# One stacked float32r product for the first feed-forward layer, finer steps beside the attention rounds, and a gather that turns two images' choices at once

## The chip, the cores and the metric

The kernel runs on one core of a Trainium2 chip. The core has a matrix engine (PE, with its weight loads PEld), a vector engine (DVE), a scalar engine for activation functions (ACT), a general engine (POOL) and SyncE (SP), which here only issues DMAs. Each engine works off its own list of instructions in order; they meet at semaphores. PE writes into PSUM[...]; the other engines read it from there. The metric is the device time of one execution in microseconds. The kernel before was timed three times: 11410.22, 11418.36 and 11421.47 us, median 11418.36.

## The reference

Four images of 64 x 64 tokens with 128 channels go through a layer of three state-space scans (forward, backward, and across slices) and then through a transformer block with a mixture of experts. What the change touches is in the second part. With 16 heads of size 8 and 4096 tokens per image:

```python
qkv = _qz_ring(heads + rx_theta)                     # q = k = v, products of cosines
scores = einsum('bhsd,bhtd->bhst', q, q) / sqrt(8)
ctx = einsum('bhst,bhtd->bhsd', softmax(scores), q)
x1 = _ln(x + ctx @ w_comb.T + b_comb, g1, beta1)
zf = cos(x1[..., :8]) * cos(ry_theta)                # 8 values a token
h = relu(zf @ w1.T + b1)                             # 8 -> 512
x2 = _ln(x1 + h @ w2.T + b2, g2, beta2)              # 512 -> 128
```

and then, on the layer norm of the sum, the experts:

```python
probs = softmax(x @ gate_w.T + gate_b, axis=tokens)  # 64 experts, each over an image's tokens
topv, topi = top_k(probs, 8)                         # 8 tokens for each expert
pooled = sum_k topv * x[topi]                        # one vector per expert and image
out = weight2(gelu(weight1(pooled)))                 # each expert's two layers
outputs[topi] += topv * out
```

## The kernel before, in words

`tile_kernel` (from L1522 on) runs in stages: the scan of image 0 beside the inputs of all images; the opening of image 0's attention; four attention loops, one per image; and a closing.

**A loop.** `loop` works through 1024 rounds (4 groups of heads x 8 query blocks x 32 key chunks). Round i issues, in this order: the four score products of round i+1 (L998, float32r, 32 rows each) with two exps of 128 x 1024 on ACT (L1003); then `beside(i)`, the place for other work; then the four value products of round i (L1012, 32 columns each, float32). PE takes them in that order, so a product that is put in by `beside` stands between the scores of the next round and the values of this one. For the first three images the scan of the next image and its opening run there, and `after` of the image before. For the last image, `by_block` is set: the rounds run query block by query block, and `self.whole[b]` counts the blocks whose context is stored.

**What runs beside the last loop**, chained in one `Pace`: `after(2)` (all eight blocks of image 2), the expert biases, search, choice and gather of images (0, 1), the same of image 2, then `after(3)` for blocks 0-3, 4-5 and 6 of image 3, each of which waits for `whole`, and the search over those seven blocks. What is left when the rounds are over is issued by `last.rest()`; then block 7 is closed (`closing`, on 7 PSUM banks), followed by choice and gather of image 3 and the experts' answers. During the loops there is a single PSUM bank for all work beside (`Bank`, size 1).

**The pace.** The parts are generators. A `yield` ends a step; `yield PE` says that the next step has PE work. In the last loop `turn(1.5, free)` allows 1.5 steps a round on average (three saved up at most), of which one PE step if `free` is true; that is `i % 3 > 0 or i > 830`. `bank.take` yields PE once. `pause()` yields PE only where `self.cut` is set, which is in the last loop.

**A block of 512 tokens.** `first(g)`: context times its share, two halves of two products with `w_comb` (`co`, L1115), norm, the first 8 channels copied to `z`. `cosines()`: range reduction on DVE and the sine on ACT, for all blocks of the call. `second(g)`: four transposes of `z` (`zt`, L1138), scaling by `cos_ry` into `zT` (8 x 512), eight products with `w1` (`h`, L1156), relu on DVE (on ACT in the closing), sixteen products with `w2` (`fo`, L1169), two norms (L878 to L884), four transposes (`xT`, L1193), two gate products (`lg`, L1207). `flow` interleaves two blocks.

**The gather.** `pool(b, g)` handles one image and four chunks of tokens: four products that turn the chosen weights (`wt`, L1342, 64 rows by 64 columns), a copy, four products with the tokens (`pool`, L1353), an addition into `pooled`.

Of the kernel before, what the change touches and what calls it, by code (L numbers as in the profile page):

```python
# [713 lines left out]
class Attention:  # L714
# [3 lines left out]
    def __init__(self, tc, ctx, w, gate, cols, ident, bank, dram, t1, w_out, scans, sz, x):  # L718
# [16 lines left out]
        self.cos_ry = const.tile([D, 3], F32, name="cos_ry")  # L735
        nc.scalar.dma_start(out=self.cos_ry[:, 0:1], in_=w["ry_theta"].unsqueeze(1))
        cosine(nc, self.cos_ry[:, 2:3], self.cos_ry[:, 0:1], self.cos_ry[:, 1:2], self.half_pi)
        self.w_comb = const.tile([P, C], F32, name="w_comb")
        self.w1 = const.tile([D, FFN], F32, name="w1")
# [6 lines left out]
        with tc.tile_pool(name="a_load", bufs=1) as load, tc.tile_pool(  # L746
# [8 lines left out]
            nc.sync.dma_start(out=raw, in_=w["w1"].rearrange("(f p) d -> p f d", p=P))  # L755
            ps = load_ps.tile([P, 512], F32, tag="ps", name="ps_w1")
            for f in range(4):
                nc.tensor.transpose(ps[:D, f * P : (f + 1) * P], raw[:, f, :], ident)
            nc.vector.tensor_copy(self.w1, ps[:D])
# [299 lines left out]
    def after(self, b, gs=range(L // QB), to=None):  # L1059
# [13 lines left out]
        z = self.small.tile([P, NT, D], F32, tag="z", bufs=1, name=f"z_{b}_{gs[0]}")  # L1073

# [20 lines left out]
        def first(g):  # L1095
# [32 lines left out]
        def second(g):  # L1128
# [12 lines left out]
            nc.vector.tensor_scalar_mul(zT, ps[:D], self.cos_ry[:, 2:3])  # L1141
# [8 lines left out]
            for f in range(4):  # L1150
                ps = yield from self.bank.take(f"h_{b}_{g}_{f}")
                for part in range(2):
                    cols = slice(part * QB // 2, (part + 1) * QB // 2)
                    if part:
                        yield from self.pause()
                    nc.tensor.matmul(ps[:, cols], self.w1[:, f * P : (f + 1) * P], zT[:, cols], start=True, stop=True)  # L1156
# [63 lines left out]
        def cosines():  # L1220
            turns = self.small.tile([P, NT, D], F32, tag="zturns", bufs=1, name=f"zturn_{b}_{gs[0]}")
            zs, turns = (t[:, 4 * gs[0] : 4 * blocks.stop, :] for t in (z, turns))
# [4 lines left out]
            yield  # L1227
            yield
# [10 lines left out]
class Experts:  # L1239
# [4 lines left out]
    def __init__(self, tc, ctx, ident, weight1, weight2, block, nb):  # L1244
# [14 lines left out]
        self.diagonal = const.tile([P, nb // 2, E], F32, name="diagonal")  # L1259
# [40 lines left out]
    def choice(self, images, blocks):  # L1300
# [24 lines left out]
        for b in images:  # L1325
            own = slice(b % 2 * E, b % 2 * E + E)
            nc.vector.tensor_scalar_mul(
                self.diagonal[own, b // 2, :], self.ident[own, own], self.share[own, b // 2 : b // 2 + 1]
# [4 lines left out]
    def pool(self, b, g):  # L1333

        nc, bank, rows = self.nc, self.block.bank, slice(b % 2 * E, b % 2 * E + E)
        x = self.some.tile([P, 4, C], F32, tag="x", bufs=4, name=f"x_{b}_{g}")
        nc.sync.dma_start(out=x, in_=self.block.xn[b][:, g * 4 : g * 4 + 4, :])
        yield
        ps = yield from bank.take(f"wt_{b}_{g}")
# [7 lines left out]
        wT = self.some.tile([P, 4, E], F32, tag="wT", name=f"wT_{b}_{g}")  # L1347
        nc.vector.tensor_copy(wT.rearrange("p i e -> p (i e)"), ps[:, : 4 * E])
        bank.leave()
        yield  # L1350
        ps = yield from bank.take(f"pool_{b}_{g}")
        for i in range(4):
            nc.tensor.matmul(ps[:, :E], x[:, i, :], wT[:, i, :], start=(i == 0), stop=(i == 3))  # L1353
        yield
        into = self.pooled[:, :, b]
        if g == 0:
            nc.vector.tensor_copy(into, ps[:, :E])
        else:
            nc.vector.tensor_add(into, into, ps[:, :E])
        bank.leave()  # L1360
        yield
# [310 lines left out]
```

## Time and profile before

The profiled execution took 11412.32 us, of which its instructions span 11410.5.

| stretch, us from the start | what | ACT busy | PE busy | PE clock |
|---|---|---|---|---|
| 0 to 2047 | scan of image 0, inputs, opening of image 0 | | | |
| 2047 to 4426 | loop of image 0 | 2321.2 of 2379 | 2128.9 | 0.98 |
| 4428 to 6794 | loop of image 1 | 2304.5 of 2366 | 2138.9 | 0.98 |
| 6799 to 9124 | loop of image 2 | 2266.7 of 2325 | 2117.2 | 0.98 |
| 9126 to 11162 | loop of image 3 | 1925.4 of 2036 | 1964.3 | 0.98 |
| 11162 to 11228 | closing of block 7 | 4.4 of 66 | 19.0 | 0.59 |
| 11228 to 11282 | choice and gather of image 3 | 6.1 of 54 | 31.1 | 0.50 |
| 11282 to 11411 | experts and output | 20.2 of 129 | 72.9 | 0.91, then 0.67 |

The busy time of PE counts pipelined products, so a high share does not say that PE is at its peak. ACT's busy time in the loops is nearly all exps: 2048 of them in 1904.7 us in the last loop. The first three loops carry the exps of a scan on ACT as well. The products of the last loop's other work, by PE's groups between 9126 and 11162: `fo` 85.4 us (240 products), `h` 72.2 (120), `wt` 28.2, `pool` 26.5, `co` 22.5, `lg` 19.4, `xT` 14.4, `zt` 12.1. A float32 product has two records in the trace, so its count there is twice the number of products.

### The profile page before, as it was taken

What the parts mean: (1) busy time and instruction counts of PE and PEld (TensorE: products, weight loads), DVE (VectorE), ACT (ScalarE), POOL (GpSimd) and SP (SyncE); (2) the same over time, 40 slices, a digit from 0 to 9 for tenths busy, and PEclk for the clock granted to TensorE, in tenths of its full rate; (3) what the DMA queues carried; (4) which work ended last, traced back from release to release, by engine and by line L of the source; (5) the groups of instructions that cost most, each with busy time, mean ns of one, the idle gap of its engine ahead of it and who ended that gap; (6) DMA issues with size and microseconds to landing.
All of it is one profiled execution on the core that took longest, in us unless ns stands there. A gap on an engine that the chain in (4) does not pass through costs nothing.

```text
span 11410.5 us, 183033 instructions
## 1 busy us (share of the span) xinstructions
PE 9874.3 (87%) x68358; PEld 3273.6 (29%) x68358; DVE 8258.3 (72%) x8405; ACT 9993.7 (88%) x10828; POOL 3790.3 (33%) x3891
## 2 busy tenths in 40 slices
PE   6687792788998889899998899999998999999995
PEld 2233331222222222222222222222222223333323
DVE  6889997888888987999988979988998321111212
ACT  4566672899999999999999999999999999989992
POOL 4777784332323223424333124243331110000000
PEclk8798895899999999999999999999999999999997
DMA  6778897656565665665656755656556332222225
GB/s 188 226 231 230 226 249 198 161 145 156 142 155 155 178 174 146 158 154 142 151 147 160 194 157 156 156 141 151 146 147 162 116 100 72 76 71 84 75 65 186
DMA packets 900980, 1747.52 MB, mean 153 GB/s; under 512 B 203150, under 2 KB 443846, under 8 KB 899830
## 3 DMA queue, kind: packets, MB, share of 16 engines
q1 hardware_dynamic: 764734, 1469.68, 47.9%
q0 software_dynamic: 93856, 156.41, 4.8%
q10 hardware_dynamic: 41496, 109.71, 3.6%
q8 instruction: 537, 8.80, 0.3%
q14 instruction: 357, 2.92, 0.1%
HBM read 1379.76 MB, written 355.47 MB: 152 GB/s over the span
## 4 chain that ended last, share of the span: by engine, by line
PE 38%; ACT 24%; issue 14%; DVE 11%; DMA 10%; POOL 1%; SPq 1%; ACTq 0%; DVEq 0%; POOLq 0%
PE acc L1012 21%; ACT e L1003 20%; PE s L998 10%; DVE h L561 5%; DMA delta<-d_delta 4%; PE cv L412 2%; DMA du<-d_du 2%; DVE dB L551 1%; ACT dA L542 1%; PE y L599 1%; ACT delta L542 1%; PE fo L1169 1%; PE xd L426 1%; PE h L1156 1%; DMA w<-in_L_ffn_weight_dram 1%
## 5 line engine op out<-in xcount | busy, mean ns | idle before, releaser
L1003 ACT ACTIVATE e<-s 128x1024 f32<-128x1024 f32 x8192 | 7778.1, 1105 | 234.2 <-PE s L998 222.2
L1012 PE MATMUL acc<-e,val 128*32 128x512 f32 x32768 | 5250.2, 615 | 106.5 <-ACT av L1021 93.7
L998 PE MATMUL s<-qm,key 32*128 32x512 f32 x16384 | 2650.8, 501 | 588.8 <-ACT e L1003 558.9
L998 PEld LDWEIGHTS s<-qm,key 32*128 32x128 f32 x16384 | 1013.4, 184 | 4444.4 <-issue 2483.9
L563 POOL COPY ends<-h 128x1 f32<-128x1 f32 x1152 | 1333.8, 1159 | 2362.4 <-DVE h L561 2353.2
L551 DVE TENSOR_TENSOR dB<-du,B 128x1024 f32<-128x1024 f32 x960 | 1213.6, 1264 | 441.2 <-PE y L599 217.2
L1012 PEld LDWEIGHTS acc<-e,val 128*32 128x32 f32 x32768 | 973.5, 109 | 1608.4 <-issue 789.0
L561 DVE TENSOR_TENSOR_SCAN h<-dA,ends,dB 128x1024 f32<-128x1024 f32 x576 | 1351.2, 2346 | 110.3 <-ACT dA L542 66.2
L542 ACT ACTIVATE dA<-delta,A 128x1024 f32<-128x1024 f32 x768 | 935.7, 1218 | 500.5 <-DMA delta<-d_delta 460.8
L561 DVE TENSOR_TENSOR_SCAN h<-delta,ends,du 128x1024 f32<-128x1024 f32 x432 | 1013.2, 2345 | 127.2 <-ACT delta L542 64.3
L568 POOL TENSOR_TENSOR hC<-h,C 128x1024 f32<-128x1024 f32 x384 | 993.5, 2588 | 153.3 <-PE y L599 83.7
L542 ACT ACTIVATE delta<-delta,A 128x1024 f32<-128x1024 f32 x768 | 937.4, 1221 | 7.3 <-DVE dB L551 2.2
L572 DVE TENSOR_TENSOR du<-h,C 128x1024 f32<-128x1024 f32 x576 | 702.2, 1219 | 0.1
L572 DVE TENSOR_TENSOR dB<-h,C 128x1024 f32<-128x1024 f32 x576 | 702.2, 1219 | 0.0
L551 DVE TENSOR_TENSOR du<-du,B 128x1024 f32<-128x1024 f32 x576 | 691.6, 1201 | 5.8 <-DMA B<-d_bc 5.8
L1027 POOL DMA_DIRECT2D d_ctx<-av x512 | 260.3, 518 | 1026.1 <-DVE av L1021 647.6
L412 PE MATMUL cv<-xn,conv 128*128 128x512 f32 x1024 | 469.7, 612 | 26.8 <-DVE xn L346 17.2
L593 POOL DMA_DIRECT2D d_du<-x_delta x272 | 157.2, 578 | 1003.0 <-DVE x_delta L592 945.1
L561 DVE TENSOR_TENSOR_SCAN h<-dA,dB 128x1024 f32<-128x1024 f32 x192 | 438.9, 2286 | 50.3 <-ACT dA L542 40.9
L599 PE MATMUL y<-hC,sel 128*32 128x256 f32 x3072 | 247.8, 456 | 171.7 <-DVE o L615 160.0
L599 PE MATMUL y<-dB,sel 128*32 128x256 f32 x4608 | 378.8, 401 | 9.9 <-DVE xT L1196 4.8
L561 DVE TENSOR_TENSOR_SCAN h<-delta,du 128x1024 f32<-128x1024 f32 x144 | 329.1, 2285 | 68.3 <-issue 35.0
(246 smaller groups left out, 7200.5 us busy)
## 6 DMA issues: line engine op xcount, KB each, us to landing
delta<-d_delta SPq DMA_DIRECT2D x768, 512.0 KB
du<-d_du SPq DMA_DIRECT2D x576, 512.0 KB
du<-d_du ACTq DMA_DIRECT2D x192, 512.0 KB
key<-d_q SPq DMA_DIRECT2D x352, 256.0 KB
d_u<-u SPq DMA_DIRECT2D x48, 1024.0 KB
d_delta<-r SPq DMA_DIRECT2D x48, 1024.0 KB
B<-d_bc SPq DMA_DIRECT2D x96, 512.0 KB
C<-d_bc SPq DMA_DIRECT2D x96, 512.0 KB
```

The source lines that it names most:

```text
L412: nc.tensor.matmul(banks[2 * m + g], w["conv"][:, k, m * P : (m + 1) * P], reads(k, g), start=(k == 0), stop=(k == 3))
L542: nc.scalar.activation(tiles["delta", s], t, AF.Exp, scale=A)
L551: nc.vector.tensor_mul(tiles["du", s], du, spread[order, c, "B", j % 2])
L561: nc.vector.tensor_tensor_scan(h, dA, dB, first, ALU.mult, ALU.add)
L563: nc.gpsimd.tensor_copy(ends[order, c][:, at : at + 1], h[:, T - 1 :])
L568: nc.gpsimd.tensor_mul(tiles["du", s], h, spread[order, c, "C", j % 2])
L572: nc.vector.tensor_mul(dB, h, spread[order, c, "C", j % 2])
L599: nc.tensor.matmul(y[32 * g : 32 * g + 32, : T // 4], self.sel[:, j // 2, :], hC[:, 256 * g : 256 * g + 256], start=(j == 0), stop=(j == 3),)
L998: nc.tensor.matmul(s_ps[:, k, :], keys[f"{i // 4}"][rows, cut].bitcast(F32R), queries[j, qb][rows, :].bitcast(F32R), start=True, stop=True,)
L1003: nc.scalar.activation(e, s_ps, AF.Exp, scale=1.0 / math.sqrt(D))
L1012: nc.tensor.matmul(accs[j, qb][32 * k : 32 * k + 32, :], v[:, k * VW : k * VW + 32], es[i][k // 2][:, k % 2, :], start=(kc == 0), stop=(kc ...
L1027: nc.gpsimd.dma_start(out=self.context[b][h * D : h * D + D, cut], in_=av[32 * k : 32 * k + D, :])
```

## The change

It has three parts.

1. The first feed-forward product. Each of `zf` and `w1` is split into a high part (the upper bits, by a mask) and a low part (the rest)[...]. They are stacked to 32 rows, `z` as high, low, high, low and `w1` as high, high, low, low. One float32r product of 32 rows and 512 columns then gives what two float32 products of 256 columns gave. `cos_ry` is multiplied into `z` before the split, by DVE in `cosines()`, rather than by the copy out of PSUM; the transposes `zt` now bring 32 rows.
2. Pauses. Inside the last loop `co` is put in one product at a time rather than two, `fo` one rather than two, and `wt` and `pool` two rather than four. The `h` product needs no pause any more.
3. The gather takes the pair of images (0, 1) in one call: `wt` uses 128 rows and 128 columns (a diagonal of 128) and makes the turned weights of both, and `pool` then follows for each image.

```diff
+def split(nc, to, src):
+    bits = mybir.dt.uint32
+    nc.vector.tensor_single_scalar(to[0].bitcast(bits), src.bitcast(bits), HIGH, ALU.bitwise_and)
+    nc.vector.tensor_sub(to[1], src, to[0])
...
-        self.w1 = const.tile([D, FFN], F32, name="w1")
+        self.w1 = const.tile([4 * D, FFN], F32, name="w1")
...
+        parts = self.one.tile([P, NT, 4, D], F32, tag="zparts", bufs=1, name=f"zparts_{b}_{gs[0]}")
...
                 for k in range(2):
+                    if k:
+                        yield from self.pause()
                     at = slice((2 * half + k) * P, (2 * half + k + 1) * P)
                     nc.tensor.matmul(ps[:, k * C : (k + 1) * C], cT[:, at], self.w_comb, start=True, stop=True)
...
-                nc.tensor.transpose(ps[:D, k * P : (k + 1) * P], z[:, g * 4 + k, :], self.ident)
+                nc.tensor.transpose(
+                    ps[: 4 * D, k * P : (k + 1) * P], parts[:, g * 4 + k, :, :].rearrange("p x d -> p (x d)"), self.ident
+                )
             yield
-            zT = self.piece([D, 512], "p0", name=f"zT_{b}_{g}")
-            nc.vector.tensor_scalar_mul(zT, ps[:D], self.cos_ry[:, 2:3])
+            zT = self.piece([4 * D, 512], "p0", name=f"zT_{b}_{g}")
+            nc.vector.tensor_copy(zT.bitcast(F32R), ps[: 4 * D])
...
-                for part in range(2):
-                    cols = slice(part * QB // 2, (part + 1) * QB // 2)
-                    if part:
-                        yield from self.pause()
-                    nc.tensor.matmul(ps[:, cols], self.w1[:, f * P : (f + 1) * P], zT[:, cols], start=True, stop=True)
+                nc.tensor.matmul(
+                    ps, self.w1[:, f * P : (f + 1) * P].bitcast(F32R), zT.bitcast(F32R), start=True, stop=True
+                )
...
                 for f in range(4):
-                    if f == 2:
+                    if f:
                         yield from self.pause()
                     nc.tensor.matmul(
                         ps[:, :C], h[:, f, k * P : (k + 1) * P], self.w2[:, f, :], start=(f == 0), stop=(f == 3)
...
             nc.scalar.activation(zs, zs, AF.Sin, bias=self.half_pi, scale=-1.0)
             yield
+            yield
+            n = zs.shape[1]
+            four = parts[:, 4 * gs[0] : 4 * blocks.stop, :, :]
+            nc.vector.tensor_mul(zs, zs, self.cos_ry[:, 2, :].unsqueeze(1).to_broadcast([P, n, D]))
+            split(nc, (four[:, :, 0, :], four[:, :, 1, :]), zs)
+            nc.vector.tensor_copy(four[:, :, 2:, :], four[:, :, :2, :])
             yield
...
-    def pool(self, b, g):
+    def pool(self, images, g):
...
         for i in range(4):
             at = (g * 4 + i) * P
+            if i == 2:
+                yield from pause()
             nc.tensor.matmul(
-                ps[:, i * E : (i + 1) * E], self.chosen[b // 2][rows, at : at + P], self.diagonal[rows, b // 2, :],
+                ps[:, i * n : (i + 1) * n], self.chosen[j][rows, at : at + P], self.diagonal[rows, j, rows],
                 start=True, stop=True,
             )
...
+        for k, (b, x) in enumerate(zip(images, xs)):
+            ps = yield from bank.take(f"pool_{b}_{g}")
+            for i in range(4):
+                if i == 2:
+                    yield from pause()
+                nc.tensor.matmul(ps[:, :E], x[:, i, :], wT[:, i, k * E : (k + 1) * E], start=(i == 0), stop=(i == 3))
...
     def gather(self, images):
-        yield from flow((self.pool(b, g) for b in images for g in range(NT // 4)), 2, 3)
+        yield from flow((self.pool(images, g) for g in range(NT // 4)), 2, 3)
```

More of the change, by code (lines that the diff above doesn't have):

```diff
@@ L734, in __init__ @@
         nc.scalar.dma_start(out=self.b1, in_=w["b1"].rearrange("(f p) -> p f", p=P))
-        self.cos_ry = const.tile([D, 3], F32, name="cos_ry")
-        nc.scalar.dma_start(out=self.cos_ry[:, 0:1], in_=w["ry_theta"].unsqueeze(1))
-        cosine(nc, self.cos_ry[:, 2:3], self.cos_ry[:, 0:1], self.cos_ry[:, 1:2], self.half_pi)
+        self.cos_ry = const.tile([P, 3, D], F32, name="cos_ry")
+        nc.scalar.dma_start(out=self.cos_ry[:, 0, :], in_=w["ry_theta"].partition_broadcast(P))
+        cosine(nc, self.cos_ry[:, 2, :], self.cos_ry[:, 0, :], self.cos_ry[:, 1, :], self.half_pi)
         self.w_comb = const.tile([P, C], F32, name="w_comb")
-        self.w1 = const.tile([D, FFN], F32, name="w1")
+        self.w1 = const.tile([4 * D, FFN], F32, name="w1")
         self.w2 = const.tile([P, 4, C], F32, name="w2")
@@ L755, in __init__ @@
             nc.sync.dma_start(out=raw, in_=w["w1"].rearrange("(f p) d -> p f d", p=P))
+            parts = load.tile([P, 4, 4, D], F32, name="parts_w1")
+            split(nc, (parts[:, :, 0, :], parts[:, :, 2, :]), raw)
+            nc.vector.tensor_copy(parts[:, :, 1, :], parts[:, :, 0, :])
+            nc.vector.tensor_copy(parts[:, :, 3, :], parts[:, :, 2, :])
             ps = load_ps.tile([P, 512], F32, tag="ps", name="ps_w1")
             for f in range(4):
-                nc.tensor.transpose(ps[:D, f * P : (f + 1) * P], raw[:, f, :], ident)
-            nc.vector.tensor_copy(self.w1, ps[:D])
+                nc.tensor.transpose(
+                    ps[: 4 * D, f * P : (f + 1) * P], parts[:, f, :, :].rearrange("p x d -> p (x d)"), ident
+                )
+            nc.vector.tensor_copy(self.w1.bitcast(F32R), ps[: 4 * D])
             raw = load.tile([P, FFN], F32, name="raw_w2")
@@ L1137, in second @@
                     yield from self.pause()
[L1138 removed]
+                nc.tensor.transpose(
+                    ps[: 4 * D, k * P : (k + 1) * P], parts[:, g * 4 + k, :, :].rearrange("p x d -> p (x d)"), self.ident
+                )
             yield
[L1140 to L1141 removed]
+            zT = self.piece([4 * D, 512], "p0", name=f"zT_{b}_{g}")
+            nc.vector.tensor_copy(zT.bitcast(F32R), ps[: 4 * D])
             self.bank.leave()
@@ L1151, in second @@
                 ps = yield from self.bank.take(f"h_{b}_{g}_{f}")
-                for part in range(2):
-                    cols = slice(part * QB // 2, (part + 1) * QB // 2)
-                    if part:
-                        yield from self.pause()
-                    nc.tensor.matmul(ps[:, cols], self.w1[:, f * P : (f + 1) * P], zT[:, cols], start=True, stop=True)
+                nc.tensor.matmul(
+                    ps, self.w1[:, f * P : (f + 1) * P].bitcast(F32R), zT.bitcast(F32R), start=True, stop=True
+                )
                 yield
@@ L1220, in cosines @@
         def cosines():
-            turns = self.small.tile([P, NT, D], F32, tag="zturns", bufs=1, name=f"zturn_{b}_{gs[0]}")
-            zs, turns = (t[:, 4 * gs[0] : 4 * blocks.stop, :] for t in (z, turns))
+            zs = z[:, 4 * gs[0] : 4 * blocks.stop, :]
+            turns = parts[:, gs[0] : blocks.stop, :, :].rearrange("p t x d -> p (t x) d")
             turned(nc, zs, turns)
@@ L1258, in __init__ @@
         self.share = const.tile([P, nb // 2], F32, name="share")
-        self.diagonal = const.tile([P, nb // 2, E], F32, name="diagonal")
+        self.diagonal = const.tile([P, nb // 2, P], F32, name="diagonal")
         self.found, self.ahead, self.rooms = {}, [], 0
@@ L1327, in choice @@
             nc.vector.tensor_scalar_mul(
-                self.diagonal[own, b // 2, :], self.ident[own, own], self.share[own, b // 2 : b // 2 + 1]
+                self.diagonal[own, b // 2, :], self.ident[own, :], self.share[own, b // 2 : b // 2 + 1]
             )
@@ L1331, in choice @@
         yield
-    def pool(self, b, g):
-        nc, bank, rows = self.nc, self.block.bank, slice(b % 2 * E, b % 2 * E + E)
-        x = self.some.tile([P, 4, C], F32, tag="x", bufs=4, name=f"x_{b}_{g}")
-        nc.sync.dma_start(out=x, in_=self.block.xn[b][:, g * 4 : g * 4 + 4, :])
+    def pool(self, images, g):
+        nc, bank, pause = self.nc, self.block.bank, self.block.pause
+        rows = slice(images[0] % 2 * E, images[-1] % 2 * E + E)
+        n, j, xs = len(images) * E, images[0] // 2, []
+        for b in images:
+            x = self.some.tile([P, 4, C], F32, tag="x", bufs=4, name=f"x_{b}_{g}")
+            nc.sync.dma_start(out=x, in_=self.block.xn[b][:, g * 4 : g * 4 + 4, :])
+            xs.append(x)
         yield
-        ps = yield from bank.take(f"wt_{b}_{g}")
+        ps = yield from bank.take(f"wt_{images[0]}_{g}")
         for i in range(4):
             at = (g * 4 + i) * P
+            if i == 2:
+                yield from pause()
             nc.tensor.matmul(
-                ps[:, i * E : (i + 1) * E], self.chosen[b // 2][rows, at : at + P], self.diagonal[rows, b // 2, :],
+                ps[:, i * n : (i + 1) * n], self.chosen[j][rows, at : at + P], self.diagonal[rows, j, rows],
                 start=True, stop=True,
@@ L1346, in pool @@
         yield
-        wT = self.some.tile([P, 4, E], F32, tag="wT", name=f"wT_{b}_{g}")
-        nc.vector.tensor_copy(wT.rearrange("p i e -> p (i e)"), ps[:, : 4 * E])
+        wT = self.some.tile([P, 4, n], F32, tag="wT", name=f"wT_{images[0]}_{g}")
+        nc.vector.tensor_copy(wT.rearrange("p i e -> p (i e)"), ps[:, : 4 * n])
         bank.leave()
         yield
[L1351 to L1361, printed above, removed]
+        for k, (b, x) in enumerate(zip(images, xs)):
[4 more added lines that the diff above has]
+                nc.tensor.matmul(ps[:, :E], x[:, i, :], wT[:, i, k * E : (k + 1) * E], start=(i == 0), stop=(i == 3))
+            yield
+            into = self.pooled[:, :, b]
+            if g == 0:
+                nc.vector.tensor_copy(into, ps[:, :E])
+            else:
+                nc.vector.tensor_add(into, into, ps[:, :E])
+            bank.leave()
+            yield
     def gather(self, images):
-        yield from flow((self.pool(b, g) for b in images for g in range(NT // 4)), 2, 3)
+        yield from flow((self.pool(images, g) for g in range(NT // 4)), 2, 3)
     def weights(self, stream, g, by):
```

## The prediction

> **What bounds the kernel now.** I read first the windows of the four attention loops (busy us of each engine, then PE clock, DMA share, GB/s), then ACT's groups inside the last loop.
>
> ```profile
> 2047.00:4426.00 2379.00, 2128.88 (x15690) 631.89 (x15686) 2042.00 (x1740) 2321.19 (x2490) 692.35 (x907) 0.98 0.60 156
> 4428.00:6794.00 2366.00, 2138.86 (x16072) 672.73 (x16076) 2101.62 (x2144) 2304.45 (x2473) 784.84 (x953) 0.98 0.60 157
> 6799.00:9124.00 2325.00, 2117.15 (x15802) 662.74 (x15800) 1931.07 (x2010) 2266.72 (x2436) 726.43 (x877) 0.98 0.57 148
> 9126.00:11162.00 2036.00, 1964.26 (x13696) 631.71 (x13692) 393.68 (x996) 1925.36 (x2079) 177.06 (x314) 0.98 0.26 76
> ```
> ```profile
> L1003 ACT ACTIVATE e<-s 128x1024 f32<-128x1024 f32 x2048 | 1904.7, 1061 | 109.2 <-PE s L998 99.1 <-ACT e L1003 0.5
> ```
>
> ACT is the bound in every loop: it idles 58, 62, 58 and 111 us. So lighter PE work can win at most those idle times, and the last loop has most of it: 109 us before the exps, 99 of them ended by a score product on PE.
>
> Next, PE's timeline in that loop: an undisturbed stretch, one with two `fo` products a round, one with four `pool` or `wt` products a round.
>
> ```profile
> 11150.78 0.50 PE L998 MATMUL s<-qm,key 32*128 32x512 f32 x4
> 11151.22 1.47 PE L1012 MATMUL acc<-e,val 128*32 128x512 f32 x8
> 11152.62 0.50 PE L998 MATMUL s<-qm,key 32*128 32x512 f32 x4
> ...
> 10990.43 0.51 PE L998 MATMUL s<-qm,key 32*128 32x512 f32 x4
> 10990.77 0.59 PE L1156 MATMUL h<-zT,w 8*128 8x256 f32 x2
> ...
> 10992.28 0.51 PE L998 MATMUL s<-qm,key 32*128 32x512 f32 x4
> 10992.72 0.71 PE L1169 MATMUL fo<-w,h 128*128 128x128 f32 x4
> 10993.36 1.07 PE L1012 MATMUL acc<-e,val 128*32 128x512 f32 x8
> 10994.36 0.50 PE L998 MATMUL s<-qm,key 32*128 32x512 f32 x4
> ```
> ```profile
> 10082.41 0.50 PE L998 MATMUL s<-qm,key 32*128 32x512 f32 x4
> 10082.84 1.10 PE L1353 MATMUL pool<-wT,x 128*128 128x64 f32 x8
> 10083.88 1.07 PE L1012 MATMUL acc<-e,val 128*32 128x512 f32 x8
> 10084.87 0.50 PE L998 MATMUL s<-qm,key 32*128 32x512 f32 x4
> ```
>
> Read the distance between score products: 1.835 us alone, 1.85 with one `h`, 2.08 with two `fo`, 2.46 with four `pool` or `wt`. Scores and values need 0.43 + 1.00 us, so about 0.4 us a round is free; whatever is longer stops ACT. Last, the stretch after the loop:
>
> ```profile
> 11175.84 0.55 DVE L1090 RECIPROCAL sum<-sum 128x64 f32<-128x64 f32 x1 [13.24 <-DMA w<-in_L_ffn_weight_dram]
> 11186.74 0.69 DVE L1107 TENSOR_TENSOR cT<-cT,part 128x512 f32<-128x512 f32 x1 [10.35 <-DMA part<-d_share]
> 11200.10 7.19 PE L1156 MATMUL h<-zT,w 8*128 8x256 f32 x16 [0.83 <-DVE zT L1141]
> 11207.23 5.79 PE L1169 MATMUL fo<-w,h 128*128 128x128 f32 x32
> 11228.10 0.76 DVE L1211 TENSOR_SCALAR prob<-lg,gate_b 64x512 f32<-64x512 f32 x1 [2.06 <-PE lg L1207]
> ```
>
> Here nothing hides anything: one block of 512 tokens goes through first() and second() as a serial chain, 42.1 us from `cT` (11186.74) to its logits (11228.86).
>
> **What the skill says.** The Trainium skill, "FP8 and Floating Point Precision", section TensorE Precision Notes: a true FP32 product takes four passes, a reduced one is read truncated. The trace agrees in direction: four float32r score products of 512 columns take 0.43 us, four float32 value products 1.00. The same skill, "TensorE: Matmul & The Clock Gate", Part 1: after an idle window of some 3.4 us PE runs at half clock. The trace agrees: clock 0.98 in the loops, 0.50 from 11170 on; four `fo` products take 0.64 us in the loop and 5.79/4 = 1.45 after it.
>
> **The change, part by part.**
>
> The first product: 8 float32 products of 256 columns per block become 4 float32r ones of 512. An `h` step of 0.52 us costs its round 0.02, so in the last loop this wins almost nothing by itself. In the second and third loop two `h` products stand beside one round (1.04 us); ACT gaps after such rounds add up to 6.8 and 5.0 us. I take 8 for both, between -10 (new order of the scan steps) and 20. The float32r product with 32 rows isn't in the trace; nearest is the score product, so 0.2 to 0.45 us: hidden either way.
>
> The cosines: per call three or four small DVE operations more (mul, and, sub, copy; 0.18 to 0.7 us by rows of that size). For 8 blocks that is about 1.7 us ahead of `zt`, which already stops PE for 1 to 2 us; four calls in the loop become three: +3 us. The weight's preparation before the loops: under 1 us.
>
> Single products beside a round. 120 rounds hold two `fo`, each 0.13 (alone) to 0.24 us long over 1.835; one `fo` (0.32) fits: 20 us won. 46 rounds of four `wt` or `pool` measure 0.57 too long on average, 26 us; two to a round (0.52) leave about 0.05 each: 23 won. `co`: 5 won, as the next half comes 3 rounds on and the bank is free.
>
> But the turns have a price. The last loop's planner lets one PE step in per round, in two of three rounds until round 830. Per block, PE steps go from 24 (co 2, zt 2, h 8, fo 8, xT 2, lg 2) to 30 (4, 2, 4, 16, 2, 2); the gathers from 48 to 80 (the pair 8 x 6, the single image 8 x 4). With 15 blocks and the biases: 15 x 24 + 49 = 409 steps before, 15 x 30 + 81 = 531 now. The instruction order of both built programs shows where they end: before, block 6's `lg` stands beside round 951 and the loop's last 70 rounds are empty. In the changed program image 2's last `lg` moves from round 452 to 557, image 3's blocks 0 to 3 end at 980 instead of 821, and when the rounds run out there are left: three `fo` of block 4, the whole of block 5 after its `zt`, and block 6 with its search. All of it runs after the loop, in series, on one PSUM bank.
>
> What that costs, from the last value product on (11161.90 in the old trace):
> - Rest of blocks 4 and 5. `fo` twice, two norms with their passes and one interleaved `h`, as 11213.34 to 11223.7 shows: 16.8. Then three `h` (0.4 PE + 0.75 DVE + handover), `xT`, four `fo` at half clock (1.8 + 0.3 + handover) and one `lg`: 18.1. Then norms, `xT`, `lg` of block 5 (15.5 in the old closing, plus handovers): 16.7. Sum 51.6.
> - Block 6. Its reciprocal to `cT` 6.85 (10943.62 to 10950.47, when it last ran), then 42.1 as the closing block, + 1.5 for `co` and + 3.6 for `fo` on one bank, + 0.8 cosines, - 1.7 for `h`: 46.3. Sum 53.2.
> - Its search: from the end of its logits to the end of MAX8 it took 11029.37 to 11043.66: 14.3. DVE does it ahead of block 7's reciprocal.
>
> 119.1 in all. Against it, block 7's own sums, which were waited for until 11175.84 (13.9 us), now arrive behind that work. So the tail gets 105.2 longer. Bounds: 85 if PE's clock stays high (about 20 products lose 0.5 to 0.9 less), 120 if each of some 30 bank handovers takes 0.3 more or DMAs are slow. Block 7 itself: `h` 4 x 0.43 in place of 7.19, with ACT's relu behind it, -4.6; cosines +0.8: -3.8.
>
> Queues that this passes: SP's seven loads of block 6 (sums, u, context, share, mid, t1, search) and POOL's stores run after the loop's last keys; behind them wait block 7's loads. ACT's queue issues the first three groups of expert weights after block 6's sine, not at 11161.90. They are needed at the first expert product, 120 us later (11281.9), and move with it.
>
> What leaves the loop with the spill: two stalls for `xT` (5.7 and 3.8 at rounds 906 and 948) and one cosine's table loads with its `zt` (4.2): 14. Loop sum: -20 - 23 - 5 - 14 + 3 = -59, bounds -40 and -75.
>
> Sum on the profiled execution (span 11410.5, execution 11412.3): -59 - 8 + 105 - 4 = +34. The median shown, 11418.4, is 6 above it; on that footing 11452.
>
> **The rivals.**
> - The stalls go too. With twice the rounds between dependent steps PE could also stop waiting for `x`, `cT` and DVE's norms. Then the loop wins 95 instead of 59, and the sum is -2: 11416, not slower. It decides from a loop gain of 93. For it: only some 45 us of the 109 are long bursts. Against: `co` still follows its share's DMA by the same rounds, the two waits for `chosen` (7 us each) and ACT's own table loads stay.
> - The spill hides behind the expert weights. From 11282 to 11349 the DMA queues are full (share 0.95); if those 67 us could begin earlier, the sum is -33: 11385. Against: only five groups fit, and each further load waits for an answer, which waits for the gather.
> - A longer spill: handovers, half clock and late weights at their dear end, little loop gain: +70 to +100, 11500.
>
> **How the numbers follow.** Forecast 0.57 (0 to +70; a few of these within 0.2%), waits gone 0.23, spill hidden 0.12, longer 0.08. 0.2% is 23 us, about what a measurement here can tell. Faster 0.12, same 0.23 + 0.10 = 0.33, slower 0.55. The range, 11408 to 11488, leaves out most of the hidden case and the top of the long one.
>
> **What would show it.** Right: `fo`, `xT` and `lg` of two blocks and a MAX8 between the last exp and the first reciprocal of the closing; 115 to 120 us from the last exp to that reciprocal in place of 14; the last loop near 1975 us with ACT idle near 60; rounds with `fo` at 1.84. Wrong: a loop under 1940, or a reciprocal less than 85 us after the last exp.

## The result, and the profile after

The changed kernel takes 11434.8 us (median of 18 runs, 11414.7 to 11444.8); the kernel before took 11410.5 us (18 runs, the three told of above among them, 11400.0 to 11428.2). The ratio is 1.0017, 95% interval 1.001 to 1.0023: a small slowdown, whose interval leaves out 1. The profiled executions differ by 22.7 us in span (11410.5 and 11433.2). Little came out of two large movements in opposite directions.

The windows of the changed kernel: the third and the last attention loop, then what lies behind the last loop (columns as before: window, length, busy us of PE, PE's weight loads, DVE, ACT and POOL with instruction counts, PE clock, DMA share, GB/s).

```profile
6800.00:9130.00 2330.00, 2117.08 (x15738) 653.00 (x15734) 1944.97 (x2023) 2269.63 (x2438) 700.58 (x883) 0.98 0.56 148
9132.00:11085.00 1953.00, 1902.75 (x13322) 581.09 (x13318) 343.68 (x863) 1908.94 (x2077) 161.99 (x289) 0.99 0.25 77
11085.00:11201.00 116.00, 37.92 (x136) 24.78 (x130) 51.84 (x142) 1.04 (x2) 17.66 (x30) 0.56 0.19 58
11201.00:11253.00 52.00, 14.84 (x56) 11.18 (x56) 20.22 (x65) 2.75 (x5) 9.73 (x17) 0.53 0.43 152
```

The last loop is 83 us shorter: 1953 against 2036. The third window has no counterpart before: 116 us in which ACT is busy for 1 us, no engine is busy for as much as half of the time, and PE's clock is 0.56. These are blocks of image 3 that no longer found a place in the loop. ACT's group for the exps and PE's groups for the work beside, both of the last loop:

```profile
L1016 ACT ACTIVATE e<-s 128x1024 f32<-128x1024 f32 x2048 | 1890.6, 1079 | 43.9 <-PE s L1011 40.5 <-ACT e L1016 0.2
```
```profile
L1185 PE MATMUL fo<-w,h 128*128 128x128 f32 x394 | 96.2, 326 | 0.0
...
L1131 PE MATMUL co<-w_comb,cT 128*128 128x128 f32 x112 | 28.0, 332 | 6.7 <-DVE cT L1121 6.3 <-DVE x L1134 0.4
L1370 PE MATMUL wt<-diagonal,chosen 128*128 128x128 f32 (+1 forms) x128 | 22.4, 297 | 6.1 <-DVE chosen L1352 6.1
L1170 PE MATMUL h<-zT,w 32*128 32x512 f32 x52 | 20.9, 402 | 6.8 <-DVE h L1175 6.8
```

The idle time ahead of the exps fell from 109.2 to 43.9 us. In PE's groups look at the counts: `fo` has 394 records instead of 480, `co` 112 instead of 120, `h` 52 products where the whole of the loop's 15 blocks would need 60. What is missing ran later. And `co` waits 0.4 us for `x` (the first half added, and with that the one PSUM bank free) where it waited 7.2 before:

```profile
L1115 PE MATMUL co<-w_comb,cT 128*128 128x128 f32 x120 | 22.5, 312 | 13.3 <-DVE x L1118 7.2 <-DVE cT L1107 6.1
```

PE's timeline shows rounds with a single `fo` and with two `pool`:

```profile
10855.15 0.50 PE L1011 MATMUL s<-qm,key 32*128 32x512 f32 x4
10855.58 0.49 PE L1185 MATMUL fo<-w,h 128*128 128x128 f32 x2
10856.00 1.07 PE L1025 MATMUL acc<-e,val 128*32 128x512 f32 x8
10856.99 0.50 PE L1011 MATMUL s<-qm,key 32*128 32x512 f32 x4
...
10341.09 0.51 PE L1011 MATMUL s<-qm,key 32*128 32x512 f32 x4
10341.53 0.66 PE L1384 MATMUL pool<-wT,x 128*128 128x64 f32 x4
10342.12 1.07 PE L1025 MATMUL acc<-e,val 128*32 128x512 f32 x8
10343.12 0.50 PE L1011 MATMUL s<-qm,key 32*128 32x512 f32 x4
```

From score product to score product it is 1.84 us with one `fo` (2.08 with two, before) and 2.03 with two `pool` (2.46 with four). So one `fo` fits beside a round, and two `pool` do not quite. Last, DVE's timeline behind the loop:

```profile
11085.58 0.69 DVE L1034 COPY av<-acc 128x512 f32<-128x512 f32 x1 [4.08 <-PE acc L1025]
11086.43 0.29 DVE L1189 TENSOR_TENSOR x1r<-x1r,fo 128x128 f32<-128x128 f32 x1 [0.16 <-PE fo L1185]
...
11133.28 0.74 DVE L1230 TENSOR_SCALAR lgs<-lg,gate_b 64x512 f32<-64x512 f32 x1 [2.06 <-PE lg L1223]
11133.94 0.53 DVE L1104 RECIPROCAL sum<-sum 128x64 f32<-128x64 f32 x1
...
11186.24 0.74 DVE L1230 TENSOR_SCALAR lgs<-lg,gate_b 64x512 f32<-64x512 f32 x1 [2.06 <-PE lg L1223]
11196.70 3.89 DVE L1314 MAX8 best<-prob 64x8 f32<-64x3584 f32 x1 [9.72 <-DMA prob<-d_lg]
11200.63 0.55 DVE L1104 RECIPROCAL sum<-sum 128x64 f32<-128x64 f32 x1
11213.93 0.69 DVE L1121 TENSOR_TENSOR cT<-cT,part 128x512 f32<-128x512 f32 x1 [12.75 <-DMA part<-d_share]
11251.75 0.76 DVE L1227 TENSOR_SCALAR prob<-lg,gate_b 64x512 f32<-64x512 f32 x1 [2.06 <-PE lg L1223]
```

The copy of `av` is the loop's end. Behind it come, one after the other, the rest of blocks 4 and 5 (to the `lgs` that ends at 11134.0: 48.5 us), block 6 (to 11187.0: 53.0), its search (MAX8 ends at 11200.6: 13.6), and only then the reciprocal of block 7, 115.1 us behind the copy where it was 13.9. From the `av` copy to `prob`, the logits of block 7, it is 166.2 us; it was 66.2.

The account of the 22.7 us, from the two traces: the last loop begins 5.9 later (9132.3 against 9126.4), its exps take 82.3 less (2033.3 to 1951.0), the way from the `av` copy to block 7's logits 100.0 more, and what follows, gather and experts, 1.0 less.

What made the loop shorter can be read from ACT's timeline. An undisturbed round of two exps takes 1.8335 us from first exp to first exp; here each round's excess over that is put down to what stood beside it. Rounds over 0.8 us too long are waits, except those in which ACT itself had something else to do; the wait for `av` is that of the first value product behind every 32nd round, which can't start until DVE has copied the old sums out of `acc`.

| excess over 1.8335 us a round, last loop, us | before | after | `e1_every_round` | `e5_only_pauses` | `e7_every_gaps` |
|---|---|---|---|---|---|
| `fo` products | 20.7 | 1.2 | 1.3 | 1.3 | 2.1 |
| `pool` and `wt` products | 25.8 | 9.2 | 9.6 | 12.1 | 9.3 |
| `co` and its waits | 23.2 | 10.3 | 15.8 | 13.3 | 6.3 |
| `h` and its waits | 13.8 | 7.1 | 1.3 | 3.1 | 0.7 |
| waits of `xT` for the norm | 20.8 | 10.6 | 21.0 | 5.6 | 0 |
| waits of `wt` for `chosen` | 14.3 | 8.2 | 14.1 | 11.7 | 0 |
| waits for the copy to `av` | 11.7 | 2.5 | 16.4 | 7.0 | 32.2 |
| ACT's own: softmax of the choice, table loads | 22.0 | 19.0 | 22.2 | 15.9 | 22.1 |
| all, with a small rest | 156.7 | 74.4 | 109.0 | 71.5 | 80.8 |

The last three columns are runs told of below. What an entry gets depends on how a round with several things in it is booked: booked by what PE runs between two score products, entries move by up to 4 us (before, `fo` is then 23.8 and `h` 10.0), while the totals stay as they are.

### The profile page after: what moved, and what is told of

Its sections match the earlier page's. It is cut to its first block, busy times and chain, and to the rows that moved or that the text cites. A ratio compares the mean times of both kernels' runs of the same rounds, so it can differ in the third digit from the quotient of the medians.

```text
span 11433.2 us, 182161 instructions
## 1 busy us (share of the span) xinstructions
PE 9837.2 (86%) x67910; PEld 3224.1 (28%) x67910; DVE 8270.8 (72%) x8429; ACT 9975.6 (87%) x10826; POOL 3740.3 (33%) x3891
## 3 DMA queue, kind: packets, MB, share of 16 engines
q1 hardware_dynamic: 764734, 1469.68, 47.5%
## 4 chain that ended last, share of the span: by engine, by line
PE 38%; ACT 23%; issue 13%; DVE 13%; DMA 10%; POOL 1%; SPq 1%; ACTq 0%; DVEq 0%; POOLq 0%
PE acc L1025 21%; ACT e L1016 19%; PE s L1011 10%; DVE h L568 6%; DMA delta<-d_delta 3%; DVE dB L558 2%; DMA du<-d_du 2%; PE cv L419 2%; ACT dA L549 1%; ACT delta L549 1%; PE fo L1185 1%; PE y L606 1%; PE xd L433 1%; DMA B<-d_bc 1%; DMA w<-in_L_ffn_weight_dram 1%
## 5 line engine op out<-in xcount | busy, mean ns | idle before, releaser
L570 POOL COPY ends<-h 128x1 f32<-128x1 f32 x1152 | 1280.5, 1112 | 2425.9 <-DVE h L568 2403.1
L575 POOL TENSOR_TENSOR hC<-h,C 128x1024 f32<-128x1024 f32 x384 | 991.2, 2582 | 166.2 <-PE y L606 81.9
L1189 DVE TENSOR_TENSOR x1r<-x1r,fo 128x128 f32<-128x128 f32 x128 | 36.1, 282 | 638.7 <-PE fo L1185 638.7
L568 DVE TENSOR_TENSOR_SCAN h<-delta,du 128x1024 f32<-128x1024 f32 x144 | 328.8, 2284 | 77.8 <-issue 43.9
```

The lines of the kernel that those rows point to most:

```text
L568: nc.vector.tensor_tensor_scan(h, dA, dB, first, ALU.mult, ALU.add)
L570: nc.gpsimd.tensor_copy(ends[order, c][:, at : at + 1], h[:, T - 1 :])
L575: nc.gpsimd.tensor_mul(tiles["du", s], h, spread[order, c, "C", j % 2])
```

## The experiments

The theory: the whole gain of the loop is made by the pauses; the whole loss is their price in PE steps, of which the pace admits one in two of three rounds; the float32r product and the turned pair matter only by the steps that they save. The first rival: the spill behind the loop isn't due to the pace, or costs nothing of its own. The second: the float32r product makes the gain. All kernels were timed beside the kernel before, five to thirteen runs each; it ran at 11413.9 us (beside the first four) and 11415.1 us (beside the others) in the median. The last columns are of one profiled execution of each, which lies up to 13.5 us from the median: the last loop is from its first to its last exp, and the tail from the last `av` copy to block 7's logits.

| run | ratio to before, 95% interval | last loop | ACT idle ahead of exps | tail |
|---|---|---|---|---|
| before | 1 | 2033.3 | 109.2 | 66.2 |
| after | 1.0017 (1.001 to 1.0023) | 1951.0 | 43.9 | 166.2 |
| `e1_every_round` | 0.9943 (0.9931 to 0.9956) | 1985.6 | 74.9 | 57.8 |
| `e2_old_steps` | 1.0004 (0.9996 to 1.0012) | 2043.9 | 120.0 | 58.4 |
| `e3_fo_in_twos` | 0.9953 (0.9941 to 0.9965) | 1999.4 | 74.0 | 58.5 |
| `e5_only_pauses` | 1.0073 (1.006 to 1.0087) | 1948.0 | 43.2 | 237.7 |
| `e6_pauses_every` | 0.9994 (0.9986 to 1.0002) | 1988.4 | 77.2 | 105.3 |
| `e7_every_gaps` | 0.9919 (0.9905 to 0.9932) | 1957.4 | 47.5 | 58.1 |
| `e8_float32_h` | 0.9973 (0.9962 to 0.9984) | 1999.7 | 83.5 | 63.0 |
| `e9_single_images` | 0.9946 (0.9933 to 0.9958) | 1977.7 | 65.9 | 55.3 |

**A PE step in every round.** The changed kernel with the pace opened; nothing is left out.

```diff
-        block.loop(nb - 1, lambda i: last.turn(1.5, i % 3 > 0 or i > 830), True)
+        block.loop(nb - 1, lambda i: last.turn(1.5, True), True)
```

> The changed kernel with one edit: in the last loop a PE step may stand beside every round, not two of three. In its instruction order block 6's last gate product is then beside round 981, so nothing of image 3's blocks 0 to 6 is left after the loop. Spill theory: the wait from the last value product to block 7's reciprocal goes from 115 us back to about 14; the loop grows by 10 to 20 (block 6 and its stalls return), so about 85 us less than the changed kernel and 60 to 65 less than before: ratio 0.994 to 0.995. Rival, that the finer steps themselves cost what is lost (or that single products in successive rounds add up and stop ACT): within 20 us of the changed kernel, ratio about 1.002, with a loop over 2010 us.

It took 11349.1 us, ratio 0.9943: 0.0074 below the changed kernel. DVE's timeline of this run at the end of the loop:

```profile
11049.98 3.89 DVE L1314 MAX8 best<-prob 64x8 f32<-64x3584 f32 x1 [9.52 <-DMA prob<-d_lg]
...
11117.62 0.69 DVE L1034 COPY av<-acc 128x512 f32<-128x512 f32 x1 [57.97 <-PE acc L1025]
11131.17 0.55 DVE L1104 RECIPROCAL sum<-sum 128x64 f32<-128x64 f32 x1 [12.85 <-DMA x<-d_un]
```

The search of the seven blocks (MAX8) ends 64 us ahead of the loop's last copy, and DVE then has nothing to do for 58 us. Block 7's reciprocal follows the copy by 13.6 us, as before the change. So the spill was the pace's, and it was a real cost. The loop itself, though, is 35 us longer than after the change, more than the spilled work should bring:

```profile
L1016 ACT ACTIVATE e<-s 128x1024 f32<-128x1024 f32 x2047 | 1890.4, 1075 | 74.9 <-PE s L1011 70.5 <-ACT e L1016 0.5
```

The table of excesses says why. The rounds with `fo`, `pool` and `wt` are as short as after the change; the waits for DVE (`co`, `xT`, `chosen`, `av`) are 67 us together where they were 32. The two traces can be split at the logits of image 3's block 3, so that the same work lies ahead of that point in both. In rounds over 0.8 us too long, these four kinds of wait then have 48 us ahead of it where the changed kernel has 29, and 16 us behind it, in blocks 4 to 6, where the changed kernel, with only the start of these blocks in its loop, has none. So about half of the rise comes with the same work at the denser pace, and the rest with work that is back in the loop. For the first half the reading is that steps follow each other without the free third round, so that PE comes to a product before DVE has its operand; no run shows that by itself.

**The change without its pauses.** The float32r product and the pair stay; `fo` and `co` go in twos, `wt` and `pool` in fours.

```diff
-                    if k:
-                        yield from self.pause()
...
-                    if f:
+                    if f == 2:
...
-            if i == 2:
-                yield from pause()
...
-                if i == 2:
-                    yield from pause()
```

> The changed kernel without its new pauses: co and fo in twos, wt and pool in fours; the stacked float32r product and the pair's gather stay. Spill theory: 341 PE steps, block 6 ends beside round 936, no spill, tail as before; bursts return, with wt of the pair now 1.3 us in one piece: loop 2010 to 2035 us, ratio 0.998 to 1.000. Rival, that the float32r product or the longer cosines cause the loss: ratio 1.001 to 1.003 as in the changed kernel.

11416.9 us, no difference from before in the interval. Nothing is spilled, and nothing is won:

```profile
L1016 ACT ACTIVATE e<-s 128x1024 f32<-128x1024 f32 x2045 | 1901.8, 1065 | 120.0 <-PE s L1011 110.3
```

ACT stands idle for 120.0 us, more than before. By the same reckoning as in the table `fo` costs 21.8 us and `pool` with `wt` 22.1, about as before; `co` with its waits costs 36.7 against 23.2, and the copy to `av` 19.1 against 11.7. The loop came out 9 to 34 us longer than expected with these waits, and the ratio just above the expected 0.998 to 1.000. A likely reason, which no run isolates: with four steps for `h` instead of eight, dependent steps come sooner, and PE waits more. The rival that the float32r product makes the gain falls here; nor is there a loss for it or the longer cosines to have caused.

**`fo` in twos, the other pauses kept.**

```diff
-                    if f:
+                    if f == 2:
```

> The changed kernel with fo in twos again, all else kept (one product of co, two of wt and pool to a step). Spill theory: 411 PE steps, block 6 ends beside round 978, no spill; fo's bursts cost 10 to 20 us more than in the changed kernel and block 6 returns to the loop (15): loop 1975 to 1990, tail 14, ratio 0.995 to 0.997. Rival, that a spill costs little and the loop's relief is what counts: slower than the changed kernel, above 1.002.

11359.6 us, ratio 0.9953. With 411 PE steps in place of 531 everything fits within the old pace. The ratio is within what was expected, the loop 9 us above it. It is 48 us longer than after the change, of which `fo` makes 21.4 (22.6 against 1.2): single `fo` products are worth that in the loop, but rounds for the 120 further PE steps had to be there.

**Only the pauses, on the kernel before.** `h` is float32 in eight products, and the gather takes one image at a time.

```diff
+                    if k:
+                        yield from self.pause()
...
-                    if f == 2:
+                    if f:
...
+            if i == 2:
+                yield from self.block.pause()
...
+            if i == 2:
+                yield from self.block.pause()
```

> The kernel before with only the pauses added (float32 h in halves, gather image by image). Spill theory: a block now takes 34 PE steps, the gathers 96, so the work runs out of rounds earlier: the end of block 3, blocks 4, 5 and 6 and the search run after the loop, 165 to 185 us from the last value product to block 7's reciprocal; the loop wins 70 to 85 as in the changed kernel: net 75 to 100 us slower than before, ratio 1.0065 to 1.009. Rival, that the pauses help and something else in the change costs: ratio below 1.000.

11500.5 us. The loop is as short as after the change, and ACT idles as little:

```profile
L1003 ACT ACTIVATE e<-s 128x1024 f32<-128x1024 f32 x2046 | 1889.5, 1075 | 43.2 <-PE s L998 39.6 <-ACT e L1003 0.3
```

So the loop gets as short without the float32r product and the pair. Not all of that is won by shorter bursts: part is work that has left the loop. With all the work inside, the change at its denser pace leaves the loop at 1985.6 us (`e1_every_round`), 48 below before. The tail is 171.5 us longer than before (237.7 against 66.2):

```profile
11074.99 0.69 DVE L1021 COPY av<-acc 128x512 f32<-128x512 f32 x1 [2.04 <-PE acc L1012]
...
11095.79 0.74 DVE L1216 TENSOR_SCALAR lgs<-lg,gate_b 64x512 f32<-64x512 f32 x1 [1.29 <-PE lg L1209]
...
11170.95 0.74 DVE L1216 TENSOR_SCALAR lgs<-lg,gate_b 64x512 f32<-64x512 f32 x1 [2.06 <-PE lg L1209]
...
11199.20 0.74 DVE L1216 TENSOR_SCALAR lgs<-lg,gate_b 64x512 f32<-64x512 f32 x1 [2.06 <-PE lg L1209]
...
11257.19 0.74 DVE L1216 TENSOR_SCALAR lgs<-lg,gate_b 64x512 f32<-64x512 f32 x1 [0.36 <-PE lg L1209]
...
11272.32 3.89 DVE L1294 MAX8 best<-prob 64x8 f32<-64x3584 f32 x1 [13.20 <-DMA prob<-d_lg]
...
11312.75 0.76 DVE L1213 TENSOR_SCALAR prob<-lg,gate_b 64x512 f32<-64x512 f32 x1 [2.06 <-PE lg L1209]
```

Four `lgs`, of blocks 3 to 6, lie behind the last `av`, up to 182 us behind it; then come the search and block 7's `prob`. The expected 165 to 185 us to block 7's reciprocal cannot be read off, because here part of block 7's opening runs among the other blocks: a reciprocal of one block's size stands at 11086.4, ahead of that of blocks 4 and 5. Block 7's logits follow the end of the search by 37 us, where it takes 51 in the changed kernel. The search ends 201 us behind the copy, so the spill is longer than expected, and the early opening takes some of it back. Against the changed kernel this run is 0.0056 slower: that is what the float32r product and the pair are worth inside the change, mostly through the 76 steps that they save (60 of `h`, 16 of the gather), for one block more is spilled. In the spilled blocks the product itself counts too: 2.07 us here in place of 0.79 for 128 of the 512 hidden values, four times a block.

**Pauses, and a step in every round, on the kernel before.** The last run's edits and the first run's line together.

> The kernel before with the pauses (float32 h in halves, gather image by image) and a PE step beside every round. A block takes 34 PE steps, so block 6 and its search alone are left after the loop. If the stacked product and the pair's gather matter only by the rounds that they save: 70 to 80 us from the last value product to block 7's reciprocal in place of 14, the loop 10 to 20 shorter than with every round and the whole change (1986), so 35 to 50 us slower than that kernel and 15 to 30 faster than before: ratio 0.9975 to 0.9985. Rival, that the stacked product takes real time off the last loop: the loop itself is 10 or more longer than 1986, ratio above 1.000.

11408.6 us, ratio 0.9994 (0.9986 to 1.0002): slower than expected. Even at one step a round there is no room: block 6 is closed behind the loop, the search ends 68 us behind the last copy, and the tail is 39 us longer than before. The loop was expected shorter as well. ACT idles 77.2 us; reckoned as in the table, long waits of `co` have 14.9 us, of `xT` 17.8, for `chosen` 16.2 and for `av` 11.6: 60 us, near the 67 of the first run and far from the 38 of these same steps at the slower pace. The expectation had taken over the waits of the slower pace. So the waits come back at the denser pace in this kernel too, and here too part of them comes with work that is back in the loop. The rival's sign, a loop of 1996 us or more, did not come (1988.4), but with block 6 outside this loop has less to do.

**Room for the waits.** The first run with empty PE steps ahead of the products that wait longest.

```diff
+    def gap(self, n):
+        for _ in range(n if self.cut else 0):
+            yield PE
...
+            yield from self.gap(3 if len(gs) == 8 else 0)
...
+            yield from self.gap(3 if g == gs[-1] else 0)
             ps = yield from self.bank.take(f"xT_{b}_{g}")
...
+        yield from self.block.gap(4)
...
-        block.loop(nb - 1, lambda i: last.turn(1.5, i % 3 > 0 or i > 830), True)
+        block.loop(nb - 1, lambda i: last.turn(1.5, True), True)
```

> The changed kernel with a PE step beside every round, and three empty PE steps ahead of the last block's xT in each call, four ahead of the gather, three ahead of the first co of image 2. Nothing else moves; block 6 still ends at round 999. If the remaining long stalls are products issued before DVE or a DMA has made their input: the loop loses about 4 x 6.5 (xT) + 2 x 7 (wt) + 5 (co) = 45 of its excess, 25 to 45 us faster than with every round alone: ratio 0.990 to 0.992. Rival, that a stall only moves to the next product of the chain: within 10 us of 0.9943.

11326.1 us, ratio 0.9919, the fastest kernel of the study, and within what was expected.

```profile
L1021 ACT ACTIVATE e<-s 128x1024 f32<-128x1024 f32 x2048 | 1890.6, 1075 | 47.5 <-PE s L1016 42.5 <-ACT e L1021 0.7
```

The loop does all the work and ACT idles hardly longer than in the changed kernel, which left most of two blocks and the end of a third for later. The waits of `xT` and for `chosen` are gone. But see who waits now; PE's group of the value products in this loop and in the changed kernel's, then PE's and DVE's timelines of this run at one of the two longest stops:

```profile
L1030 PE MATMUL acc<-e,val 128*32 128x512 f32 x8190 | 1289.3, 613 | 32.1 <-DVE av L1039 32.0
...
L1025 PE MATMUL acc<-e,val 128*32 128x512 f32 x8192 | 1312.8, 610 | 9.3 <-DVE av L1034 8.9
```
```profile
11033.17 0.50 PE L1016 MATMUL s<-qm,key 32*128 32x512 f32 x4
11039.28 1.93 PE L1030 MATMUL acc<-e,val 128*32 128x512 f32 x8 [5.61 <-DVE av L1039]
```
```profile
11037.51 1.12 DVE L902 TENSOR_SCALAR x1r<-t,mv_x,rs_x 128x128 f32<-128x128 f32 x4 [1.44 <-POOL rs_x L51]
11038.54 0.68 DVE L1039 COPY av<-acc 128x512 f32<-128x512 f32 x1
```

The value products of a new key group wait 5.61 us for DVE's copy to `av`. The copy stands in DVE's queue behind a whole norm, which for its part waits 1.44 us for POOL. By PE's group this wait is 32.0 us in all; in the changed kernel it was 8.9. So of the 44.6 us that the empty steps won at `co`, `xT` and `chosen` against the first run, 15.8 came back at `av`: the rival, a stall that moves, holds for about a third. The reading is that the empty steps shift the norms into rounds where copies are due; the two longest stops show it, the shorter ones were not followed up.

**`h` in float32, as one step.** The first run with the two float32 products of 256 columns, on the same 32 rows, in place of the float32r one; the number of steps is the same.

```diff
-                nc.tensor.matmul(
-                    ps, self.w1[:, f * P : (f + 1) * P].bitcast(F32R), zT.bitcast(F32R), start=True, stop=True
-                )
+                for part in range(2):
+                    cols = slice(part * QB // 2, (part + 1) * QB // 2)
+                    nc.tensor.matmul(ps[:, cols], self.w1[:, f * P : (f + 1) * P], zT[:, cols], start=True, stop=True)
```

> The changed kernel with a PE step beside every round, and h as two float32 products of 256 columns in one step, on the same 32 stacked rows: same steps, same order, only the product's kind differs. If h's length counts where it is over the 0.4 us that a round leaves: 60 rounds in the last loop with 1.04 us in place of 0.49 cost 0.55 each, 25 to 35 us, and 5 to 12 in the second and third loop: 30 to 45 slower than with every round, ratio 0.997 to 0.998. Rival, that PE's h time is hidden: within 10 us of 0.9943.

11385.1 us: 0.0030 slower than the first run. PE's timelines, first of this kernel, then of `e1_every_round`:

```profile
9461.29 0.50 PE L1011 MATMUL s<-qm,key 32*128 32x512 f32 x4
9461.62 1.02 PE L1172 MATMUL h<-zT,w 32*128 32x256 f32 x4
...
9463.57 0.51 PE L1011 MATMUL s<-qm,key 32*128 32x512 f32 x4
```
```profile
10981.90 0.50 PE L1011 MATMUL s<-qm,key 32*128 32x512 f32 x4
10982.24 0.39 PE L1170 MATMUL h<-zT,w 32*128 32x512 f32 x1
...
10983.73 0.50 PE L1011 MATMUL s<-qm,key 32*128 32x512 f32 x4
```

The same work is 1.02 us in float32 and 0.39 in float32r. The first makes its round 2.28 us long, the second leaves it at 1.83; these are also the medians over the 60 rounds with `h`. Those rounds have 21.0 us of excess in this run's last loop and 1.3 in the first run's. By the spans the difference is 28.5 us. The last loop has 14 of it, since its waits became shorter by some 6; the tail has 5, where block 7 is closed with the slower product; and the last loop starts 9.6 later.

**Images turned one at a time, with pauses.** The first run with the gather as it was, in the new steps.

```diff
-        yield from flow((self.pool(images, g) for g in range(NT // 4)), 2, 3)
+        yield from flow((self.pool((b,), g) for b in images for g in range(NT // 4)), 2, 3)
```

> The changed kernel with a PE step beside every round, gathering one image at a time with the pauses kept (64 rows, 64 columns to a wt product, as before): 16 PE steps more, block 6 ends at round 1017, still inside. If the pair's gather matters only by steps: within 8 us of every round alone, ratio 0.9935 to 0.995. Rival, that 128 rows and columns at once save PE time that counts: 10 us or more slower.

11356.5 us, ratio 0.9946 beside the first run's 0.9943, each in the other's interval. Turning two images at once saves 16 steps, and where there is room for these it saves no time that can be measured here.

## Why the prediction was right, and what was off

The forecast was 34 us on the profiled execution, with one sign and one cause; it came to 22.7 (24.3 by the medians), by the same cause. The total is closer than its terms. The last loop won 23 us more than its -59, and it began 6 us later where the two loops ahead of it were to win 8. These misses have opposite signs, and 14 of the 23 us cancelled by luck.

- **The spill** was foreseen block by block, and the trace gives each step: 51.6 for the rest of blocks 4 and 5 (measured 48.5), 53.2 for block 6 (53.0), 14.3 for the search (13.6), less 13.9 for block 7's sums. From the last `av` to block 7's reciprocal the forecast was 119; it is 115. Run `e1_every_round` shows by its removal that it costs this much.
- **Block 7 itself** became 1.1 us shorter (53.0 to 51.9 from reciprocal to logits), not 3.8: it waits 12.75 us for `part`, in a stretch in which expert weights are loaded and the DMA engines are full (share 1.02 from 11204 to 11214). In five runs with the stacked product and nothing spilled the wait is 6.5 to 7.0, and block 7 is 8 us shorter than before; with float32 `h` in the same order (`e8_float32_h`) it is 2. So the product is worth 6 us here, more than its -4.6, and in the changed kernel the waits for DMAs took it back.
- **The loop** is where a size was off: the sum of -59, with bounds -40 and -75, measured -82, outside its own bounds. Of its terms `fo` is near (-20; -19.5 in the table), the relief of the bursts was put too high (-23; -16.6, since two `pool` still take 2.03 us), and what leaves with the spill nearly right (-14 for `xT`, table loads and `zt`, +3 for longer cosines; -10.2 for `xT`, and -3.0 for ACT's own work). The terms that failed are the waits for DVE and the lighter `h`: `co` was put at -5 and gave -12.9; `h` at almost nothing, -6.7 (-3 in the other booking); `chosen` at nothing, -6.1; the copy to `av` was not thought of, -9.2. That is 35 where 5 were expected. The reading that more rounds between the steps gave DVE time for the operands fits `e1_every_round`, where the same steps at the denser pace have `chosen` at 14.1 and `av` at 16.4 again; that run has more work in its loop as well.
- **The signs it named.** The 115 us, the MAX8 ahead of block 7's reciprocal and the rounds of 1.84 us came; the loop near 1975 us with ACT idle near 60 did not (1951 and 43.9).
- **The second and third loop** were to win 8 us; they did not. From first to last exp the two take 4697 us together against 4689. Kernels that are alike in these loops differ by up to 11 us from one profile to the next, but there is no sign of a gain: 4681 to 4689 in the three with the old first product (before, `e5_only_pauses`, `e6_pauses_every`), 4686 to 4697 in the six with the new one. `e8_float32_h`, with the long product in the new order, has 4696. So the new order of the steps or the longer cosines seem to cost more than the lighter product won; which of them was not tested.
- **The rival "the stalls go too"** came more than half true: for the loop its -95 was nearer to -82 than the forecast's -59 was, but it needed -93 to decide. **"The spill hides behind the expert weights"** is refuted: gather and experts behind block 7's logits took 180.7 us against 181.7, so they moved with the spill as a whole. The longer spill did not come in the changed kernel, but did in `e5_only_pauses`.
- **A reading that was wrong.** In the line at 10992.72 four records are two `fo` products, so 0.64 us is the time of two; four take 1.28 in the loop, against 1.45 in the line behind it. That line also mixes two clocks: PE's clock is 0.50 from 11170 to 11210, and 0.84 from 11210 to 11220. `h` shows the half clock better, with 0.52 us a product in the loop and 7.19/8 = 0.90 behind it. In the changed kernel four `fo` take 2.08 us at clock 0.50 (from 11112.37) and 1.16 at clock 1.00 (from 11117.03). The 1.8 us that the sum took for four `fo` was thus a little low; it did not decide anything, as the 48.5 us show.
- The runs settle which part of the change did what. `e2_old_steps` has neither gain nor loss without the pauses, `e5_only_pauses` has both with nothing else, and `e1_every_round` keeps more than half of the loop's gain and drops the loss. The float32r product is worth 0.0030 where the whole fits (`e8_float32_h`).

What stays open: why the same steps wait longer at the denser pace, what the second and third loop lose, and whether the copy to `av` can be had ahead of the norms in DVE's queue, which would be worth up to 32 us in `e7_every_gaps`; it was not tried.

## What to carry to other kernels

Where work is fitted beside a loop under a quota of steps, count the steps times the rounds per step before splitting them: a split that makes every round shorter also needs more rounds, and what doesn't fit comes back as a serial chain, here at 0.56 of PE's clock and with every latency bare. Shorter steps and a wider quota belong to one change: the shorter steps alone cost 0.2 to 0.7% here, and with the wider quota and the lighter product they won 0.6%. After that, what is left in the loop is not length but order: empty steps ahead of products with a long wait gave another 0.2%, and moved part of the wait to another instruction in the same queue.

## What the runs showed of the hardware that was not expected

- A stop of ACT costs more than the idle time that the profile shows. The exps' records are 1.06 to 1.08 us long in the mean but follow each other every 0.917 us in an undisturbed stretch, so they overlap by some 0.15 us, and each stop loses that overlap too. In the loop before, 203 stops with 109.2 us of idle made the exps 137.5 us late; after, 68 stops with 43.9 us made them 52.8 late: 0.14 and 0.13 us a stop beyond the idle time. The rest of the 156.7 and 74.4 us is in the main ACT's own other work.
- A float32 product of 64 columns is hardly cheaper on PE than one of 128: two `pool` of 64 columns are busy for 0.66 us and make a round of 2.03, two `fo` of 128 columns 0.71 and 2.08. One `fo`, with as many columns as two `pool`, is 0.49 and leaves the round at 1.84.
- One float32r product of 32 rows and 512 columns costs 0.4 us in the timeline where two float32 products of 256 columns, over the same rows, cost 1.02.
